# Background products in quarters with pauses behind each filled bank, and block 0's halves stored once

## The chip, the cores and the metric

The kernel runs on one core of a Trainium2 chip. The time is that of one execution on the device in microseconds (us), and it is compared by the median of several runs. One more execution is taken by the hardware profiler, and all lines of the profile come from that one. The engines are named as in the profile: PE is the matrix engine (PEld its weight loads), DVE the vector engine, ACT the scalar engine with its activation functions, POOL the general engine beside them, and SP the engine that issues most of the DMAs.

## The reference

The input x is 4096 tokens of 256 features. The kernel computes a causal attention with 16 heads of 16 features, its projection, a layernorm with the residual, and then a feed-forward part with ternary weights, again with layernorm and residual. All of it is in float32.

```python
def attn(x, w_attn, b_attn, w_proj, b_proj):
    q, k, v = jnp.split(x @ w_attn + b_attn, 3, axis=-1)      # 16 heads of 16
    logits = jnp.einsum('bhqd,bhkd->bhqk', q, k) * hd ** (-0.5)
    logits = jnp.where(causal[None, None, :, :], logits, -jnp.inf)
    weights = jax.nn.softmax(logits, axis=-1)
    return jnp.einsum('bhqk,bhkd->bhqd', weights, v) @ w_proj + b_proj
...
x = x + _layernorm(attn(_layernorm(x)))
x = x + _layernorm(ffn(_layernorm(x)))      # w1, w2: 1024 hidden; h1, h2: gelu; w3
```

## The kernel before

**Blocks, items, steps, units.** The 4096 queries are cut into 8 blocks j of 512 (`NB`, `QB`), the 16 heads into 4 groups g of 4 (`G`). An item is a pair (j, g), and the items run in order. `steps(j)` (L876) gives 4j + 3 steps to an item, one for each 128 keys up to the diagonal. A step has two units, each with the scores of two heads (128 keys by 512 queries), in two banks of PSUM; the last step of an item has one. That makes 32j + 20 units for a block and 1056 in all. The scores are computed with keys and queries as sums of a rounded part (hi) and a rest (lo).

**What a unit needs.** PE makes the scores s (`products`, L843), DVE takes one maximum mx over them (L852, which guards the shift of the softmax), ACT takes the exponential e_s (L859), POOL zeroes what is above the diagonal in the last steps (L866), and PE multiplies with the values (av, L930), a few units later. Scores have three tiles of two banks.

**Background work.** Beside the attention, other jobs advance a little in each step; `bg.even(every)` (called at the end of a step, if j < 2 or the step is ahead of the diagonal) moves them. A job is a generator that yields what it needs next: `PE` or `HALF` for a piece with matrix products, `ACT` for one with statistics on ACT, others for pieces that always run. The jobs are:

- `prep(j + 2)`, added at step 2 of group 1 of block j: loads x, layernorm by statistics on ACT (the tile junk, L203 and L211) and on POOL, transposes pt (L633), which ACT evicts to xT; then for c = 0, 1 the features pk and pq (L525), which ACT evicts to full (L534), which are split to hi and lo (L542, L544: on DVE for blocks 0 and 1, on POOL for later ones) and stored to DRAM (L549); then v (pv, L650, evicted by ACT at L658).
- `project(j)`: the projection py (L314, evicted by ACT at L332) of a finished block, then mean, spread and residual y (L224 and L351 on POOL).
- `norm_block(0)` in block 7, the entry to the feed-forward part.
- `halving`, in each fourth step: ternary weights are rounded in POOL (L1009 to L1012).

Background products use one PSUM bank (pool `ps_m`, one buffer). A bank of pk, pq, pv or py is filled in two halves: 128 by 512 for each of two parts of the contraction for pk and pq, two tokens' tiles by 256 for pv and py. The transposes fill a bank in one piece. While a bank is half full, only its own job may go on (`open`). The argument `every` is 1, 1, 2, 2, 3, 3, 3, 3 for the eight blocks: one half each `every` steps, an ACT piece in the step before.

**Keys and queries.** The stored halves of a block lie in DRAM as (head, 2, 2, 16, 512): each of hi and lo is stored twice, so that one load (`load_rows`, L557) brings a tile of 128 rows that has all combinations of hi and lo for two heads. `queries` and `keys` issue the loads on SP's queue. Before group 3 of a block the q of the next block must be stored (else `bg.step()` runs until it is), and before group 0 the whole prep of the block.

**Start.** Blocks 0 and 1 are loaded and normalised; then `biases()` scales the biases of q and k and adds the v bias through the projection to bp (products pb, L1106, which need the weights wp); then come the transposes of block 0, its pk and pq for c = 0, their stores, loads of the first two items, and the rest of block 0. `prep(1)` stands in the background from the first step on.

**The end.** After the attention the feed-forward part follows (L1358 and on, 672.10 us), which the change doesn't touch.

Of the kernel before, what the change touches and what calls it, by code (L numbers as in the profile page):

```python
# [3 lines left out]

# [6 lines left out]
F32 = mybir.dt.float32  # L11
F32R = mybir.dt.float32r
AF = mybir.ActivationFunctionType
ALU = mybir.AluOpType
# [3 lines left out]
P = 128  # L18
QB = 512
NT = QB // P  # L20
# [9 lines left out]
class Background:  # L30
# [6 lines left out]
    def __init__(self, beside=lambda: None):  # L37
        self.work = deque()
        self.beside = beside
        self.at = 0  # L40
        self.open = None

    def piece(self, gen):

# [47 lines left out]
                self.run(job)  # L92
            clear = clear and not job[4]

    def even(self, every):


        self.at += 1
        pe, act = not self.at % every, not (self.at + 1) % every
        for job in list(self.work):  # L100
            if job[3] in (self.PE, self.HALF):
                if pe and self.open in (None, job):
                    pe = False
                    self.run(job)
                    self.open = job if job[3] == self.HALF else None
            elif job[3] != self.ACT:
                self.run(job)
            elif act:
                act = False
                self.run(job)  # L110
# [7 lines left out]
def sandwich_kernel(  # L118
# [154 lines left out]
    def project(j, room):  # L273
# [35 lines left out]
        for half in range(0, NT, 2):  # L309
            ps = room.bank(f"py_{j}_{half}").rearrange("p (t f) -> p t f", t=2)  # L310
            for t in range(2):
                yield room.within(t)
                for c in range(DC):
                    nc.tensor.matmul(  # L314
                        ps[:, t, :],
                        lhsT=oT[:, c, (half + t) * P : (half + t + 1) * P],
                        rhs=wp[:, c, :],
                        start=(c == 0),
                        stop=(c == DC - 1),
                    )  # L320
# [83 lines left out]
    def attention(shared):  # L404
# [8 lines left out]
        with ExitStack() as actx:  # L413
# [22 lines left out]
            class Room:  # L436


                def within(self, n):
                    return Background.HALF if shared and n else Background.BESIDE  # L440

                def bank(self, name):
                    return bank(name) if shared else two_banks(name)[:, 0, :]
# [31 lines left out]
            def constants():  # L475
# [35 lines left out]


            halves_of = {
                (s, j): scratch.tile([H, 2, 2, HD, QB], F32, tag=f"{s}_{j}", name=f"{s}_{j}")
                for s in "kq"
                for j in range(NB)
            }
# [1 line left out]
            def features(j, s, c, engine):  # L519

                i = "qk".index(s)
                ps = room.bank(f"p{s}_{j}_{c}")
                for d in range(DC):
                    yield room.within(d)
                    nc.tensor.matmul(  # L525
                        ps,
                        lhsT=wqk[d][:, i * D + c * P : i * D + (c + 1) * P],
                        rhs=xTs[j][:, d, :],
                        start=(d == 0),
                        stop=(d == DC - 1),  # L530
                    )
# [12 lines left out]
                engine.tensor_tensor(lo.bitcast(F32R), full, hi.bitcast(F32R), ALU.subtract)  # L544
                for half, part in enumerate((hi, lo)):
                    for d in range(2):
                        at = (d, half) if i else (half, d)
                        queue = nc.gpsimd if shared and j < 2 and half else nc.sync
                        queue.dma_start(  # L549
                            out=halves_of[s, j][8 * c : 8 * (c + 1), at[0], at[1]], in_=part  # L550
                        )
                stored.add((s, j, c))

            def load_rows(tag, name, key, j, h):

                t = (piece if key == "k" else query)(tag, name, F32R)
                nc.sync.dma_start(  # L557
                    out=t.bitcast(F32),
                    in_=halves_of[key, j][h : h + 2].rearrange("h a b d n -> (h a b d) n"),
                )  # L560
                return t

            def query(tag, name, dtype):
# [10 lines left out]
            RING = 2 * NB  # L574
            kT, asked = {}, [0]

            def keys(n, c):

                for pr in range(2):
                    kT[n, c, pr] = load_rows(  # L580
                        f"k{asked[0] % RING}_{pr}", f"k{n}_{c}_{pr}", "k", c, 4 * (n % G) + 2 * pr
                    )
                asked[0] += 1

# [14 lines left out]
            def prep(j, engine=nc.gpsimd):  # L599
# [30 lines left out]
                for c in range(DC):  # L630
                    ps = room.bank(f"pt_{j}_{c}")
                    for t in range(NT):
                        nc.tensor.transpose(  # L633
                            ps[:, t * P : (t + 1) * P], xj[:, t, c * P : (c + 1) * P], ident
                        )
                    lent.append(True)
                    nc.scalar.copy(xT[:, c, :], ps)
                    if shared or c == DC - 1:
                        yield Background.PE
# [5 lines left out]
                for half in range(0, NT, 2):  # L645
                    ps = room.bank(f"pv_{j}_{half}").rearrange("p (t f) -> p t f", t=2)
                    for t in range(2):
                        yield room.within(t)
                        for c in range(DC):
                            nc.tensor.matmul(  # L650
                                ps[:, t, :],
                                lhsT=xT[:, c, (half + t) * P : (half + t + 1) * P],
                                rhs=wv[:, c, :],
                                start=(c == 0),
                                stop=(c == DC - 1),
                            )
# [443 lines left out]
            issued = now = 0  # L1100

            def biases():
                nc.vector.tensor_scalar(bqk[:, 0:DC], bqk[:, 0:DC], SCALE, None, ALU.mult)
# [145 lines left out]
    def feed_forward(halves, xT0, W):  # L1249
# [6 lines left out]
        with ExitStack() as fctx:  # L1256
# [10 lines left out]
                return ap.bitcast(F32R) if halves else ap  # L1267

            class Room:
                def within(self, n):  # L1270
                    return Background.BESIDE
# [236 lines left out]
```

## Time and profile before

| | us |
|---|---|
| median of 3 runs (2049.6 to 2054.11) | 2053.32 |
| profiled execution | 2048.42 |
| its span | 2046.5 |
| start, to the first maximum (39.81) | 39.81 |
| block 0 | 53.03 |
| block 1 | 75.08 |
| block 2 | 107.02 |
| block 3 | 147.81 |
| block 4 | 185.73 |
| block 5 | 216.71 |
| block 6 | 253.81 |
| block 7 | 295.40 |
| rest and feed-forward part | 672.10 |

A block is counted from its first maximum on DVE to the first of the next. In the span PE is busy for 89%, DVE for 79%, ACT for 68% and POOL for 27%, but in the feed-forward part PE has nearly all and DVE half. For the attention the lines that matter are those of DVE, ACT and PE in one step; a busy share does not show which one waits. Rows of a timeline have a start, a length from the first start to the last end of a run of equal instructions, the engine, the line, the operation and its tiles (result before the arrow), and in brackets the idle time ahead of it and what ended it. PE's rows are pipelined, so a record is longer than the spacing of two: the products of pv have records of 0.38 us and four of them take 1.06. Each float32 product makes two records.

### The profile page before, as it was taken

How to read it: one execution, taken by the hardware profiler on the slowest of the kernel's cores; microseconds unless marked ns; L12 is line 12 of the kernel's file. 1: busy time of each engine (PE TensorE's matmuls, PEld its weight loads, DVE VectorE, ACT ScalarE, POOL GpSimd, SP SyncE). 2: the span in 40 equal slices, each digit the busy share in tenths (PEclk: the TensorE clock that was granted, in tenths of full speed). 3: DMA queues.
4: the chain of work that ended last, by engine and by line, in shares of the span. 5: the costliest groups of instructions: out<-in, count | busy, mean ns of one | idle time of the engine just before them, and what ended most of it. 6: DMA issues, size and time to landing. Idle time of an engine off the chain costs nothing.

```text
span 2046.5 us, 28401 instructions
## 1 busy us (share of the span) xinstructions
PE 1825.3 (89%) x10518; PEld 932.5 (46%) x10518; DVE 1609.8 (79%) x1894; ACT 1399.2 (68%) x1598; POOL 552.2 (27%) x871
## 2 busy tenths in 40 slices
PE   4799989988888888888888887889999999999997
PEld 2333332322322322223222222228888888888886
DVE  3689998998999999999999999985546456465453
ACT  2699999999999999999999998982212222222221
POOL 3264545434435335333333110000120000000000
PEclk8899999999999999999999998999999999999999
DMA  6756645444235333553234213103100000000000
GB/s 168 229 179 219 191 133 180 147 154 159 98 131 183 116 103 124 161 163 115 76 136 156 98 44 101 63 9 114 53 11 21 15 7 21 1 21 21 1 11 15
DMA packets 134909, 202.09 MB, mean 99 GB/s; under 512 B 16064, under 2 KB 60736, under 8 KB 134752
## 3 DMA queue, kind: packets, MB, share of 16 engines
q1 hardware_dynamic: 130496, 194.56, 29.3%
q0 software_dynamic: 2480, 4.35, 1.0%
q8 instruction: 87, 1.43, 0.3%
q10 hardware_dynamic: 1776, 1.18, 0.3%
q14 instruction: 70, 0.57, 0.1%
HBM read 137.91 MB, written 62.13 MB: 98 GB/s over the span
## 4 chain that ended last, share of the span: by engine, by line
PE 46%; ACT 21%; DVE 19%; issue 6%; DMA 4%; POOL 2%; SPq 1%; ACTq 0%; POOLq 0%; DVEq 0%
PE z L1358 21%; ACT e_s L859 19%; DVE mx L852 18%; PE av L930 7%; PE s L843 7%; PE za L1358 3%; PE zb L1358 2%; PE pyf L1440 2%; DMA k<-k 1%; PE py L314 1%; PE pk L525 1%; PE pv L650 1%; PE pq L525 1%; ACT junk L211 1%; DMA q<-hiq 0%
## 5 line engine op out<-in xcount | busy, mean ns | idle before, releaser
L852 DVE TENSOR_REDUCE mx<-s 128x1 f32<-128x1024 f32 x1056 | 1219.8, 1217 | 72.1 <-PE s L843 66.6
L859 ACT ACTIVATE e_s<-s,shift 128x1024 f32<-128x1024 f32 x1056 | 1153.6, 1117 | 104.9 <-DVE mx L852 81.9
L843 PE MATMUL s<-q,k 64*128 64x512 f32 (+3 forms) x2304 | 517.7, 468 | 161.2 <-ACT e_s L859 144.7
L930 PE MATMUL av<-e_s,v 128*32 128x512 f32 (+2 forms) x4576 | 572.8, 575 | 7.9 <-POOL e_s L866 5.7
L843 PEld LDWEIGHTS s<-q,k 64*128 64x128 f32 x2304 | 208.9, 185 | 752.9 <-ACT e_s L859 652.2
L1425 ACT ACTIVATE fb<-z,sh 128x512 f32<-128x512 f32 x128 | 88.1, 689 | 364.8 <-PE z L1358 340.2
L1358 PE MATMUL z<-hb_0l,h 128*128 128x512 f32 x512 | 199.5, 390 | 0.0
L1358 PE MATMUL z<-hb_0h,h 128*128 128x512 f32 x512 | 199.5, 390 | 0.0
L866 POOL TENSOR_SCALAR_AFFINE_SELECT e_s<-e_s 128x256 f32<-128x256 f32 (+1 forms) x224 | 94.7, 440 | 337.4 <-ACT e_s L859 337.4
L233 POOL TENSOR_TENSOR rstd<-ve,neghalf 128x4 f32<-128x4 f32 (+1 forms) x22 | 20.8, 944 | 608.8 <-DVE ve L231 603.0
L930 PEld LDWEIGHTS av<-e_s,v 128*32 128x32 f32 x4576 | 97.2, 109 | 151.5 <-issue 116.1
L1325 DVE CAST hb_1h<-fb 128x512 fp32r<-128x512 f32 x64 | 27.4, 428 | 155.7 <-ACT fb L1425 155.7
L1402 ACT ACTIVATE sl<-za,s 128x512 f32<-128x512 f32 x64 | 44.0, 690 | 120.4 <-PE za L1358 60.9
L1325 DVE CAST hb_0h<-fb 128x512 fp32r<-128x512 f32 x64 | 28.1, 440 | 99.6 <-ACT fb L1425 99.6
L1358 PEld LDWEIGHTS z<-hb_0h,h 128*128 128x128 f32 x512 | 96.1, 188 | 20.0
L1358 PEld LDWEIGHTS z<-hb_0l,h 128*128 128x128 f32 x512 | 96.2, 188 | 19.8
L1011 POOL TENSOR_SCALAR wc<-wc 128x256 f32<-128x256 f32 x88 | 75.8, 861 | 7.8
L1010 POOL TENSOR_TENSOR wc<-wc,wh 128x256 f32<-128x256 f32 x88 | 64.3, 730 | 7.2
L1012 POOL TENSOR_TENSOR fit<-fit,wc 128x256 f32<-128x256 f32 x88 | 64.2, 730 | 7.3
L1009 POOL CAST wh<-wc 128x256 fp32r<-128x256 f32 x88 | 35.0, 397 | 108.4 <-DMA wc<-in_h_t_dram 75.9
L1440 PE MATMUL pyf<-w,hb_1l 128*128 128x256 f32 x256 | 61.8, 284 | 0.0
L1440 PE MATMUL pyf<-w,hb_1h 128*128 128x256 f32 x256 | 61.7, 283 | 0.0
(257 smaller groups left out, 1970.3 us busy)
## 6 DMA issues: line engine op xcount, KB each, us to landing
k<-k SPq DMA_DIRECT2D x288, 256.0 KB
q<-q SPq DMA_DIRECT2D x64, 256.0 KB
x<-in_x_dram SPq DMA_DIRECT2D x16, 512.0 KB
k<-hik SPq DMA_DIRECT2D x32, 256.0 KB
q<-hiq SPq DMA_DIRECT2D x32, 256.0 KB
wc<-in_h_t_dram SPq DMA_DIRECT2D x64, 128.0 KB
r_h<-wh SPq DMA_DIRECT2D x64, 128.0 KB
h<-r_h SPq DMA_DIRECT2D x32, 256.0 KB
```

What stands on the lines that cost most here:

```text
L843: nc.tensor.matmul(self.both[:, i, col : col + n], lhsT=kT[G * j + g, c, pr][r, tt * P : (tt + 1) * P], rhs=qT[j, g][pr][r, QB - n :], sta ...
L852: nc.vector.tensor_reduce(next(columns), self.both.rearrange("p a n -> p (a n)"), AX.X, ALU.max)
L859: nc.scalar.activation(e, self.both, AF.Exp, bias=shifts[j])
L866: nc.gpsimd.affine_select(out=here, in_=here, compare_op=ALU.is_ge, fill=0.0, base=0, pattern=[[0, here.shape[1]], [1, P]], channel_multip ...
L930: nc.tensor.matmul(self.av[h * HW : (h + 1) * HW, QB - n :], lhsT=vb[kt // NT][:, kt % NT, o : o + HW], rhs=of(es, h), start=(kt == 0 or k ...
L1010: nc.gpsimd.tensor_tensor(w, w, hi, ALU.subtract)
L1011: nc.gpsimd.tensor_scalar(w, w, 0.0, None, ALU.is_equal)
L1012: nc.gpsimd.tensor_tensor(fit, fit, w, ALU.mult)
L1325: nc.vector.tensor_copy(hi, full)
L1358: nc.tensor.matmul(ps, lhsT=w[c], rhs=single(part[:, c, :]), start=(c == 0 and i == 0), stop=(c == kc - 1 and i == parts - 1),)
L1425: nc.scalar.activation(h, z, AF.Gelu, scale=sc[:, oc : oc + 1])
L1440: nc.tensor.matmul(ps[:, 0:D], lhsT=single(part[:, c, t * P : (t + 1) * P]), rhs=(w3_r if halves else w3_sb)[:, c, :], start=(c == 0 and i ...
```

## The change

**The rate.** `even` takes four numbers. `products` is how many pieces with products may run in a step, `every` as before, `acts` the distance between ACT pieces, `rest` the pause behind a filled bank: for that many steps after the one that filled it, counted by `at`, no product is issued (a piece may run again when `at` reaches `at + rest`, so two whole steps and the one that filled lie ahead of it), and in the step that fills a bank no ACT piece runs. The call gives, for blocks 0 to 7, products 2, 2, 2, 1, 1, 1, 1, 1; every 1, 1, 2, 1, 1, 1, 1, 1; acts 1, 1, 2, 2, 3, 3, 3, 2; rest 0, 0, 0, 3, 3, 3, 3, 3.

**The quarters.** A bank is filled in four pieces. pk and pq are cut in two by columns (128 by 256) and each cut has its two parts of the contraction; pv and py have one product in a piece; the transposes have two pieces of two. The number of matrix instructions grows by that of the cut features, one more product for each half.

**Block 0.** Its hi and lo are stored once: q as (head, 2, 16, 512), k as (head, 16, 2, 512), and the loads repeat the rows by a broadcast; a key tile of block 0 is loaded by two DMAs of 128 KB in place of one of 256. For later blocks the layout in DRAM has another order of its dimensions with the same bytes and numbers of DMAs.

**The start.** The first two key loads go to POOL's queue. The scaling of the biases stays where it was, the products pb go behind the work on block 0. Ahead of the first attention step the background runs until k of block 1, c = 0, is stored: both transposes and pk of block 1. Before the norm of block 0 in block 7, `project(6)` is finished explicitly.

```diff
-    def even(self, every):
+    def even(self, products, every, acts, rest):
         self.at += 1
-        pe, act = not self.at % every, not (self.at + 1) % every
+        pe = 0 if self.at % every or self.at < self.rested else products
+        act = self.at % acts == 1 % acts
         for job in list(self.work):
             if job[3] in (self.PE, self.HALF):
-                if pe and self.open in (None, job):
-                    pe = False
+                while pe and job[3] in (self.PE, self.HALF) and self.open in (None, job):
+                    pe -= 1
                     self.run(job)
                     self.open = job if job[3] == self.HALF else None
+                    if rest and not self.open:
+                        pe, act, self.rested = 0, False, self.at + rest
...
             ps = room.bank(f"p{s}_{j}_{c}")
-                for d in range(DC):
-                    yield room.within(d)
+                cuts = 2 if shared else 1
+                for n, (cut, d) in enumerate(product(range(cuts), range(DC))):
+                    yield room.within(n)
+                    at = slice(cut * QB // cuts, (cut + 1) * QB // cuts)
                     nc.tensor.matmul(
-                        ps,
+                        ps[:, at],
                         lhsT=wqk[d][:, i * D + c * P : i * D + (c + 1) * P],
-                        rhs=xTs[j][:, d, :],
+                        rhs=xTs[j][:, d, at],
...
+                    queue = nc.gpsimd if shared and j < 2 and half else nc.sync
+                    kept = halves_of[s, j][8 * c : 8 * (c + 1)]
+                    for d in range(2) if j else ():
                         at = (d, half) if i else (half, d)
-                        queue = nc.gpsimd if shared and j < 2 and half else nc.sync
+                        queue.dma_start(out=kept[:, at[0], :, at[1]], in_=part)
+                    if not j:
+                        queue.dma_start(out=kept[:, :, half] if i else kept[:, half], in_=part)
...
+                elif key == "k":
+                    for i in range(2):
+                        rows = part[i : i + 1].rearrange("u d b n -> u (d b) n")
                         queue.dma_start(
+                            out=to[i * P // 2 : (i + 1) * P // 2],
+                            in_=rows.broadcast_to([2, 2 * HD, QB]),
                         )
+                else:
+                    rows = part.rearrange("h a (d u) n -> (h a d) u n", u=1)
+                    queue.dma_start(out=to, in_=rows.broadcast_to([P // 2, 2, QB]))
...
                     for t in range(NT):
+                        if shared and t == NT // 2:
+                            yield Background.HALF
                         nc.tensor.transpose(
...
-            biases()
+            nc.vector.tensor_scalar(bqk[:, 0:DC], bqk[:, 0:DC], SCALE, None, ALU.mult)
             while ("q", 0, 0) not in stored:
                 bg.piece(works[0])
             for n in range(2):
                 queries(*items[n])
-                keys(*chunks[n])
+                keys(*chunks[n], nc.sync if n or not shared else nc.gpsimd)
             while bg.piece(works[0]) is not False:
                 pass
+            biases()
             if shared:
                 bg.add(("prep", 1), works[1], PREP)
                 bg.work[0][3] = Background.PE
+                while ("k", 1, 0) not in stored:
+                    bg.step()
...
+                    bg.finish(("project", NB - 2))
                     bg.add(("norm", 0), norm_block(0, room, first_features), NORM)
...
-                        bg.even(1 + j // 2 - j // 6)
+                        bg.even(1 + (j < 3), 1 + (j == 2), (1, 1, 2, 2, 3, 3, 3, 2)[j], 3 * (j > 2))
```

More of the change, by code (lines that the diff above doesn't have):

```diff
@@ L2 @@
 from contextlib import ExitStack
-from itertools import chain, cycle
+from itertools import chain, cycle, product
 import concourse.bass as bass
@@ L41, in __init__ @@
         self.open = None
+        self.rested = 0
     def piece(self, gen):
@@ L311, in project @@
             for t in range(2):
-                yield room.within(t)
                 for c in range(DC):
+                    mark = room.within(DC * t + c, c > 0)
+                    if mark:
+                        yield mark
                     nc.tensor.matmul(
@@ L436, in attention, with within @@
             class Room:
-                def within(self, n):
-                    return Background.HALF if shared and n else Background.BESIDE
+                def within(self, n, fine=False):
+                    if shared:
+                        return Background.HALF if n else Background.BESIDE
+                    return None if fine else Background.BESIDE
                 def bank(self, name):
@@ L513, in attention @@
             halves_of = {
-                (s, j): scratch.tile([H, 2, 2, HD, QB], F32, tag=f"{s}_{j}", name=f"{s}_{j}")
+                (s, j): scratch.tile(
+                    [H, 2, HD, 2, QB] if j else [H, HD, 2, QB] if s == "k" else [H, 2, HD, QB],
+                    F32,
+                    tag=f"{s}_{j}",
+                    name=f"{s}_{j}",
+                )
                 for s in "kq"
@@ L545, in features, with load_rows @@
                 for half, part in enumerate((hi, lo)):
-                    for d in range(2):
+                    queue = nc.gpsimd if shared and j < 2 and half else nc.sync
+                    kept = halves_of[s, j][8 * c : 8 * (c + 1)]
+                    for d in range(2) if j else ():
                         at = (d, half) if i else (half, d)
-                        queue = nc.gpsimd if shared and j < 2 and half else nc.sync
+                        queue.dma_start(out=kept[:, at[0], :, at[1]], in_=part)
+                    if not j:
+                        queue.dma_start(out=kept[:, :, half] if i else kept[:, half], in_=part)
+                stored.add((s, j, c))
+            def load_rows(tag, name, key, j, h, queue=nc.sync):
+                t = (piece if key == "k" else query)(tag, name, F32R)
+                to, part = t.bitcast(F32), halves_of[key, j][h : h + 2]
+                if j:
+                    queue.dma_start(out=to, in_=part.rearrange("h a d b n -> (h a d b) n"))
+                elif key == "k":
+                    for i in range(2):
+                        rows = part[i : i + 1].rearrange("u d b n -> u (d b) n")
                         queue.dma_start(
-                            out=halves_of[s, j][8 * c : 8 * (c + 1), at[0], at[1]], in_=part
-                        )
[L552 to L560, printed above, removed]
+                            out=to[i * P // 2 : (i + 1) * P // 2],
+                            in_=rows.broadcast_to([2, 2 * HD, QB]),
+                        )
+                else:
+                    rows = part.rearrange("h a (d u) n -> (h a d) u n", u=1)
+                    queue.dma_start(out=to, in_=rows.broadcast_to([P // 2, 2, QB]))
                 return t
@@ L575, in attention, with keys @@
             kT, asked = {}, [0]
-            def keys(n, c):
+            def keys(n, c, queue=nc.sync):
                 for pr in range(2):
                     kT[n, c, pr] = load_rows(
-                        f"k{asked[0] % RING}_{pr}", f"k{n}_{c}_{pr}", "k", c, 4 * (n % G) + 2 * pr
+                        f"k{asked[0] % RING}_{pr}",
+                        f"k{n}_{c}_{pr}",
+                        "k",
+                        c,
+                        4 * (n % G) + 2 * pr,
+                        queue,
                     )
@@ L647, in prep @@
                     for t in range(2):
-                        yield room.within(t)
                         for c in range(DC):
+                            mark = room.within(DC * t + c, c > 0)
+                            if mark:
+                                yield mark
                             nc.tensor.matmul(
@@ L1102, in biases @@
             def biases():
-                nc.vector.tensor_scalar(bqk[:, 0:DC], bqk[:, 0:DC], SCALE, None, ALU.mult)
                 ps = two_banks("pb")[:, 0, 0:D]
@@ L1269, in feed_forward, with within @@
             class Room:
-                def within(self, n):
-                    return Background.BESIDE
+                def within(self, n, fine=False):
+                    return None if fine else Background.BESIDE
                 def bank(self, name):
```

## The prediction

> **What bounds the kernel now.** I read the list of costly groups first, then the timeline of DVE in blocks without disturbance, then the chain of waits beside it, then the table of windows by block, and last the places where a block loses much at once.
>
> ```profile
> L852 DVE TENSOR_REDUCE mx<-s 128x1 f32<-128x1024 f32 x1056 | 1219.8, 1217 | 72.1 <-PE s L843 66.6
> L859 ACT ACTIVATE e_s<-s,shift 128x1024 f32<-128x1024 f32 x1056 | 1153.6, 1117 | 104.9 <-DVE mx L852 81.9
> ...
> 1096.80 24.91 DVE L852 TENSOR_REDUCE mx<-s 128x1 f32<-128x1024 f32 x22
> ```
>
> Main attention is 1056 units, and each needs one maximum on DVE. Twenty-two of them run without a gap in 24.91 us: (24.91 - 1.22) / 21 = 1.13 us each, so a step of two units cannot be shorter than 2.26 us. The last column says that DVE's idle time ends when PE delivers scores. A stage is therefore measured by what it takes over 1.13 us for a unit. In block 4:
>
> ```profile
> 485.51 5.75 DVE L852 TENSOR_REDUCE mx<-s 128x1 f32<-128x1024 f32 x5 [0.21 <-PE s L843]
> 491.45 1.23 DVE L852 TENSOR_REDUCE mx<-s 128x1 f32<-128x1024 f32 x1 [0.19 <-PE s L843]
> 492.88 5.75 DVE L852 TENSOR_REDUCE mx<-s 128x1 f32<-128x1024 f32 x5 [0.20 <-PE s L843]
> ...
> 488.50 0.99 PE av L930 x8
> 489.49 0.43 PE s L843 x2
> 489.92 1.06 PE pv L650 x4
> 490.98 0.43 PE s L843 x2
> ```
>
> Here a background half is issued in every third step. The cycle from 485.51 to 492.88 is 7.37 us; three free steps are 6.78. So a half costs 0.59 us. The chain shows why: PE needs 0.43 + 0.99 + 0.43 = 1.85 us for a step, which leaves 0.41 of 2.26, and the half takes 1.06. It stands between two pairs of score products, so both following maxima come late.
>
> ```profile
> 0.00:39.81 39.81, 16.28 (x46) 8.40 (x46) 11.02 (x35) 6.37 (x9) 17.11 (x31) 0.96 0.60 156
> 39.81:92.84 53.03, 39.91 (x212) 17.32 (x212) 29.00 (x34) 30.02 (x41) 16.95 (x38) 0.77 0.72 222
> ...
> 36.00:54.00 18.00, 11.62 (x44) 5.44 (x48) 6.94 (x8) 6.33 (x7) 3.37 (x8) 0.53 0.73 253
> 74.00:85.00 11.00, 7.90 (x32) 3.59 (x32) 4.24 (x8) 5.02 (x8) 3.15 (x6) 0.54 0.86 259
> ...
> 23.86 9.77 DMA q<-hiq
> 35.21 5.63 DMA k<-k
> 40.88 0.82 PE s L843 x2
> ```
>
> Columns are length, then busy time of PE, weight loads, DVE, ACT, POOL, then granted clock, DMA share and GB/s. The start ends on the store of hiq and the load of k. Block 0 has 20 units, 22.6 us of maxima, and takes 53.03. In two stretches the clock is half, and the DMA engines are three quarters full. The blocks 3 to 7 have 116, 148, 180, 212 and 244 units; by the same table they last 147.81, 185.73, 216.71, 253.81 and 295.40, which is 82 us over their maxima. Followed step by step along DVE, 36.4 of these 82 stand at the 74 halves issued there (0.49 each; block 3 and steps that had slack lose less than 0.59), 7 at ACT's statistics (junk) in other steps, and the rest at fixed places: shift and its transpose, the reciprocals, the norm in block 7, and stalls like this one:
>
> ```profile
> 346.00 0.72 POOL L1012 TENSOR_TENSOR fit<-fit,wc 128x256 f32<-128x256 f32 x1
> 346.68 2.79 POOL L866 TENSOR_SCALAR_AFFINE_SELECT e_s<-e_s 128x256 f32<-128x256 f32 x7
> ...
> 347.15 2.28 PE L930 MATMUL av<-e_s,v 128*32 128x512 f32 x8 [1.82 <-POOL e_s L866]
> ...
> 350.20 3.49 DVE L852 TENSOR_REDUCE mx<-s 128x1 f32<-128x1024 f32 x3 [3.23 <-PE s L843]
> ```
>
> At the end of an item the diagonal selects queue on POOL behind rounding of features and weights; the product av waits, and DVE stands 3.23 us.
>
> **Quarters in blocks 3 to 7.** Before, a bank (two halves) loses 2 x 0.49 = 0.98 us. After, the built order has 138 spaced quarters, which fill 34.5 banks; eight transposed banks; and four quarters that are issued together ahead of (block 3, group 3), since q of block 4 isn't stored by then. The trace has no quarter. Its nearest rows are pv, two products of 256 columns in 1.06 us, and pk, one of 512 in 1.06: so a quarter is b = 0.53. Then a step with a quarter is 1.85 + 0.53 = 2.38, 0.12 over 2.26. Four in a row lose 0.48, and I add 0.11 for the eviction by ACT, which lies in a step of its own: c = 4 (b - 0.41) + 0.11 = 0.59 per bank. The three steps behind it are there to recover the lag. 34.5 x 0.59 = 20.4; transposes 8 x 0.15 = 1.2 (a whole one takes 0.59, two transposes 0.3, under the spare 0.41); the 7 of junk stays; the forced group 2.0 (4 x 0.53). Sum 30.6, against 36.4 + 7 = 43.4: **-12.8**. Bounds: quarters wholly hidden in the spare 0.41 and the score buffers, only evictions left, 5.2 + 10.2 = 15.4, which is -28; quarters that lose in proportion to the halves, 34.5 x 0.98 + 10.2 = 44, which is +0.6. I take the value between, since 0.53 exceeds 0.41.
>
> The Trainium skill speaks against the 0.53: "TensorE: Matmul & The Clock Gate", section "Back-to-back issue gap", gives a sustained spacing of about 81 ns at 128 columns and 131 at 512, so that half the columns cost much more than half. Between its two figures, 256 columns would be some 98 (an estimate from that page), and a quarter 1.06 x 98 / 131 = 0.79 in place of 0.53; the sum of all terms would then end near 2059. The rows of pv and pk, both 1.06, disagree with it at these sizes.
>
> **POOL's selects.** The slower rate changes what lies on POOL at each diagonal. Before, four ends lose 3.32 (block 3, group 1), 3.16 (4, 0), 1.65 (2, 3) and 0.85 (4, 3): 9.0. In the new order the last three have nothing queued in front; the first still has 7 us of rounding; four other ends (3, 2), (4, 1), (5, 2), (5, 3) have 4 to 4.6 us issued a step ahead, mostly done by then. I leave 3.5 + 0.5: **-5**. Bounds -8 (the first clears too) and 0 (the new ones take over).
>
> **Start.** Half of block 0's stores go (eight of 256 KB), four of which precede the first scores, and the bias product no longer heads PE's queue: it waits for wp until 12.24 and takes 2.05, so the transposes begin near 11, not 14.42. Against it: the transposes and pk of block 1 (0.87 + 0.67 + 2.00 by the start's own rows) are now ahead of the first score on PE, its rounding (0.43 + 0.69) ahead of the first maximum on DVE; lok_1_0 needs the lo buffer of k_0_1, whose store is on POOL behind the first key loads, moved there; a store from POOL lands in 7 us. They end near 36 to 37 by my chain; the first maximum then stands at 37.3, not 39.81: **-2.5**. Bounds: -6 (all 3.5 us of the wp wait and half of the 9.77 pass through, less the new products) and +3 (one more POOL landing is exposed, half of 7).
>
> **Block 0.** Work of block 1 is gone from its first steps, and PE isn't idle for 5 us before them. At full clock the 11.62 us of PE at 0.53 would be 6.2, the 7.90 at 0.54 would be 4.3: 5.4 + 3.6 = **-9**. Bounds: -13 (also 2.35 + 1.04 of waits for k at 79.45 and 92.30) and -3 (one third; the clock stays low). The keys' loads in two DMAs of 128 KB instead of one of 256 add 64 issues on SP, beside 0.4 us each at the start: 26 us of SP's queue over 1300, which has no work in most steps; if that cover is gone, a key comes 0.4 late, once per item.
>
> **Blocks 1 and 2.** Two quarters in one step are the same products as a half: **-0.5**, bounds -2 and +2 (the cut of features reloads weights, 0.19 a time, beside the products).
>
> `bg.finish(("project", 6))` finds it done. FFN isn't touched: 0.
>
> **Sum.** -12.8 - 5 - 2.5 - 9 - 0.5 = -29.8. The profiled execution took 2048.4, its span 2046.5; the median shown is 4.9 above it. 2048.4 - 29.8 + 4.9 = **2023.5**. Root of the squares of the distances to the bounds: 16 down (3.5, 4, 1.5, 3, 15.2), 17 up (5.5, 6, 2.5, 5, 13.4).
>
> **Rivals.**
> *Quarters bring nothing* (0.15). A step with a quarter has no slack, so every eviction and every junk becomes visible, and a bank loses what two halves did. For it: junk shows 7 us already. Against: y and v evictions behind a half cost nothing more. -17 + 0.6 = -16.4: **2037**.
> *Start and block 0 give nothing* (0.10). The key loads on POOL's queue come late and the clock stays at half. For it: POOL's landing of 7 us; against: fewer bytes. +3 - 3 + 2 - 5 - 12.8 = -15.8: **2037.5**. Both together (0.05): +3 - 3 + 2 - 5 + 0.6 = -2.4, **2051**, no change.
> *A lone quarter does not stream* (0.10), the slower side. Its two passes are records of 0.38 each; end to end they are 0.76, and the score pair behind takes 0.50 as after a wait, not 0.43: b = 0.83. Then c = 1.79, 34.5 x 1.79 + 10.2 = 72, +28.6 instead of -12.8: -17 + 28.6 = +11.6, **2065**. It decides from b = 0.75 (no change) and makes it slower from 0.78. Against it: pairs of two score products stream in 0.43.
> That the change doesn't do what it says I exclude: the quarters stand apart in the built order.
>
> **Numbers.** The forecast has 0.60; its own range is 2012 to 2034. With the rivals, 8 in 10 lie in 2007 to 2042. About 0.2% (4.1 us) can be told from no change: faster 0.85, same 0.05, slower 0.10.
>
> **What would show it.** In block 4, DVE rows should show four steps near 2.38 and then steps at 2.26, quarter records at 0.53 spacing, and a block shorter by about 6; no 3 us stall at the end of (4, 0); a forced group of pq ahead of (3, 3). In the start, the first maximum near 37 and a granted clock over 0.9 from 40 to 54. Wrong it is if a step with a quarter takes over 2.6 us, if the first maximum is later than 40, or if new waits for POOL's selects stand at (3, 2), (4, 1), (5, 2) or (5, 3).

## The result, and the profile after

The changed kernel takes 2109.45 us (median of 4 runs, 2104.31 to 2110.86), against 2053.72 for the kernel before: a ratio of 1.0269, 95% interval 1.0245 to 1.0293. It is slower by 56 us, where 30 us less were forecast. The profiled execution has a span of 2108.6.

The first view is the table of windows by block (length, busy times of PE, weight loads, DVE, ACT and POOL, then granted clock, DMA share, GB/s). The rows are the start, blocks 0, 1, 2, block 4, and a stretch of 8 us inside block 0.

```profile
0.00:51.17 51.17, 22.66 (x80) 15.58 (x80) 12.31 (x36) 8.23 (x12) 17.46 (x31) 0.91 0.48 126
51.17:113.55 62.38, 38.45 (x210) 19.38 (x210) 27.92 (x33) 26.10 (x31) 15.33 (x33) 0.74 0.49 144
113.55:210.50 96.95, 76.18 (x454) 30.31 (x454) 63.69 (x62) 69.95 (x95) 39.61 (x70) 0.88 0.48 149
210.50:334.50 124.00, 103.77 (x642) 37.64 (x642) 99.93 (x92) 100.36 (x126) 49.23 (x78) 0.93 0.51 162
478.90:661.60 182.70, 169.56 (x1046) 55.44 (x1046) 173.57 (x157) 171.50 (x196) 78.67 (x123) 0.98 0.45 139
...
100.50:108.50 8.00, 4.58 (x21) 2.21 (x22) 2.10 (x2) 2.23 (x2) 0.81 (x2) 0.50 0.13 49
```

By stage, after less before: start +11.4, block 0 +9.3, block 1 +21.8, block 2 +17.1, block 3 -3.5, block 4 -3.0, block 5 +7.1, block 6 -3.9, block 7 +5.8; in sum 62. So 59.6 of these 62 us lie in the start and the first three blocks, where the background rate is the same as before. The last row shows what it is like there: DVE works 2.1 of 8 us, the clock is at half, and the DMA engines are busy for a share of 0.13, as much as 2 of 16 at full use, at 49 GB/s. The waits say who is waiting (total, times, longest), for PE and DVE:

```profile
PE s L877 <- DMA k<-k: 20.6, 9, 3.4
...
DVE hik L557 <- DMA k<-hik: 15.8, 1, 15.8
DVE least L291 <- DMA sums<-avd: 10.7, 2, 5.4
```

The timeline of SP's queue in that time (start, time from the first issue to the end of the last, line):

```profile
96.57 9.37 SPq L579 DMA_DIRECT2D k<-k  x4
106.06 3.15 SPq L575 DMA_DIRECT2D k<-k  x2
111.49 0.32 SPq L992 DMA_DIRECT2D avd<-av_sb  x1
```

L579 is the load of a key tile of block 0 in two parts, L575 that of a key tile of block 1 in one. Four issues of L579 hold SP for 9.37 us, and the two behind them for 3.15. Most issues of L579 are short (median 0.51 us), and the kernel before had held ones too (four whole tiles in 6.29 us at 81.53); how the same four tiles fare without these loads is shown below. The store of the finished attention (avd) stands behind them, so its sums come late and DVE waits for them, 5 us in each of blocks 1 and 2.

The start ends on another thing. The chain of waits there (start, length, what):

```profile
35.64 2.76 SPq L579
38.40 0.05 issue
38.47 0.03 issue
38.50 11.54 DMA k<-hik
50.03 0.03 issue
50.08 0.04 issue
50.13 0.44 DVE hik L557
50.56 0.02 issue
50.59 0.69 DVE lok L559
51.28 2.28 DVE mx L886 x2
```

The first maximum stands on DVE behind hik of block 1, which waits until the store of block 0's second hik has left their common buffer; that store is issued behind the query and key loads on SP and then takes 11.54 us.

Last the quarters, in PE's timeline of block 4:

```profile
550.41 0.50 PE L877 MATMUL s<-q,k 64*128 64x512 f32 x2
550.84 0.70 PE L540 MATMUL pq<-xT,wqk 128*128 128x256 f32 x2
551.47 0.50 PE L877 MATMUL s<-q,k 64*128 64x512 f32 x2
551.89 1.06 PE L964 MATMUL av<-e_s,v 128*32 128x512 f32 x8
552.89 0.50 PE L877 MATMUL s<-q,k 64*128 64x512 f32 x2
553.32 0.70 PE L540 MATMUL pq<-xT,wqk 128*128 128x256 f32 x2
```

From 550.84 to 551.47 a quarter holds PE for 0.63 us, not 0.53, and the step from 550.84 to 553.32 is 2.48 long.

### The profile page after: what moved, and what is told of

Read it like the earlier page. It is cut to its first block, busy times and chain, and to the rows that moved or that the text cites. A ratio compares the mean times of both kernels' runs of the same rounds, so it can differ in the third digit from the quotient of the medians.

```text
span 2108.6 us, 28718 instructions
## 1 busy us (share of the span) xinstructions
PE 1868.0 (89%) x10646; PEld 959.3 (45%) x10646; DVE 1609.9 (76%) x1894; ACT 1399.1 (66%) x1598; POOL 553.9 (26%) x871
## 4 chain that ended last, share of the span: by engine, by line
PE 44%; ACT 23%; DVE 14%; DMA 8%; issue 7%; POOL 2%; SPq 2%; ACTq 0%; POOLq 0%; DVEq 0%
ACT e_s L893 21%; PE z L1395 20%; DVE mx L886 12%; PE av L964 7%; PE s L877 6%; PE za L1395 2%; PE zb L1395 2%; PE pyf L1477 2%; DMA k<-k 2%; DMA avd<-av_sb 2%; DMA k<-hik 1%; PE py L320 1%; PE pv L684 1%; DMA x<-x 1%; PE pk L540 1%
## 5 line engine op out<-in xcount | busy, mean ns | idle before, releaser
L877 PE MATMUL s<-q,k 64*128 64x512 f32 (+3 forms) x2304 | 537.3, 475 | 172.9 <-ACT e_s L893 136.5
L964 PE MATMUL av<-e_s,v 128*32 128x512 f32 (+2 forms) x4576 | 580.5, 583 | 7.4 <-POOL e_s L900 5.2
```

What stands on the lines that cost most here:

```text
L877: nc.tensor.matmul(self.both[:, i, col : col + n], lhsT=kT[G * j + g, c, pr][r, tt * P : (tt + 1) * P], rhs=qT[j, g][pr][r, QB - n :], sta ...
L964: nc.tensor.matmul(self.av[h * HW : (h + 1) * HW, QB - n :], lhsT=vb[kt // NT][:, kt % NT, o : o + HW], rhs=of(es, h), start=(kt == 0 or k ...
```

## The experiments

Three parts can be told apart: the storing and loading of block 0 (K), the new start (S), and quarters with pauses (Q). The kernel before has none of them, the changed one all. In the expectations, theory A is at first: the loads of block 0's keys have an outer dimension of 2 and so use few DMA engines; in later ones it is what they say. Stages are taken from one profiled execution each. All runs keep the changed order of the dimensions in DRAM. One of them, with quarters from block 4 on and otherwise the old start, has blocks 1 to 3 within 0.1 us of the kernel before, but its start at 42.51 instead of 39.81, so a difference of 2 or 3 us in a start alone can't be put down to one part.

**K alone.** From the changed kernel S and Q are taken back: the bias product stands ahead of the rest of block 0 again, and banks are filled in halves by the old `even`.

```diff
-                keys(*chunks[n], nc.sync if n or not shared else nc.gpsimd)
+                keys(*chunks[n])
...
-                while ("k", 1, 0) not in stored:
-                    bg.step()
...
-                        bg.even(1 + (j < 3), 1 + (j == 2), (1, 1, 2, 2, 3, 3, 3, 2)[j], 3 * (j > 2))
+                        bg.even(1 + j // 2 - j // 6)
```

> The kernel before with one part alone: block 0's halves stored once and its keys loaded by two DMAs with a repeated outer dimension of 2. Theory A (these loads use few DMA engines, about 50 GB/s as in 100 to 112 us of the changed kernel, and hold SP's queue): blocks 0 to 2 are longer by 35 to 55 us in sum, blocks 3 to 7 as before, total 2090 to 2110. Rival B (the new order of the start delays blocks 0 to 2): no change here, 2045 to 2056. Rival C (the quarters do it): no change here either.

Measured: 2138.84, ratio 1.0428 (1.0394 to 1.0462). The start is at 41.02, blocks 0 to 2 take 72.5, 104.4 and 124.8, which is 66.6 more than before. Blocks 3 to 7 were expected as before, but are 21 us longer: 2.5, 5.3 and 5.9 of it are new at three ends of items, and 7.0 at the norm of block 7, where DVE waits 6.9 us for a load of x that stands behind key loads on SP. K alone costs more than the whole change loses; A holds as to the main place, its size was guessed too low and its reach too short.

**S alone.** K and Q are taken back in the same way.

> The kernel before with the new start alone (bias product later, first keys on POOL's queue, transposes and pk of block 1 ahead of the first scores). Theory A: start and block 0 gain a little or lose a little, total 2040 to 2055. Rival B: the first maximum at 45 to 51 and blocks 0 to 2 longer by 30 to 48, total 2090 to 2110. Rival C: no change.

Measured: 2050.44, 0.9983 (0.997 to 0.9995). The first maximum comes at 49.42 as rival B said, but blocks 0 to 2 do not suffer (47.1, 76.0, 105.6). The new start moves 6 us of block 0 ahead of the first maximum and gains next to nothing.

**All but K.** Block 0 is stored twice, its tiles are loaded by one DMA:

```diff
-                    for d in range(2) if j else ():
+                    for d in range(2):
...
-                    if not j:
-                        queue.dma_start(out=kept[:, :, half] if i else kept[:, half], in_=part)
...
-                elif key == "k":
...
+                queue.dma_start(out=to, in_=part.rearrange("h a d b n -> (h a d b) n"))
```

> The changed kernel without its part on block 0: halves stored twice and loaded by one DMA of 256 KB. Theory A: the 60 us lost in the start and blocks 0 to 2 are gone but for 5, total 2035 to 2058. Rivals B and C: the total stays over 2090.

Measured: 2040.55, 0.9945 (0.9924 to 0.9966). The 69 us between this and the changed kernel are K: 5.7 in the start, 14.5, 20.8 and 18.2 in blocks 0 to 2, 11.4 in blocks 3 to 7. The place of the stretch shown above (there the 16th maximum starts at 100.15 and the 18th at 110.12) lies here between 84.91 and 89.90. The window around it, and the loads of the same four tiles on SP's queue, now read:

```profile
82.00:90.00 8.00, 5.92 (x32) 2.93 (x36) 2.45 (x3) 3.33 (x6) 0.82 (x2) 0.57 0.61 207
...
82.01 2.27 SPq L572 DMA_DIRECT2D k<-k  x4
```

The four tiles hold SP for 2.27 us and not for 9.37 + 3.15, and the two maxima take 4.99 us and not 9.97. The clock is near half here as well (0.57), so at this place it is no sign of K.

**Is it the shape of the load?** Two kernels ask this from both sides. In the first, block 0 stays stored once, and each key tile is loaded by four DMAs with 32 rows in front:

```diff
-                    for i in range(2):
-                        rows = part[i : i + 1].rearrange("u d b n -> u (d b) n")
-                        queue.dma_start(
-                            out=to[i * P // 2 : (i + 1) * P // 2],
-                            in_=rows.broadcast_to([2, 2 * HD, QB]),
-                        )
+                    for i in range(4):
+                        rows = part[i // 2].rearrange("d b n -> (d b) n")
+                        queue.dma_start(out=to[i * P // 4 : (i + 1) * P // 4], in_=rows)
```

> The changed kernel, but a key tile of block 0 is loaded by four DMAs of 64 KB, each with 32 rows as its outer dimension, in place of two of 128 KB with a repeated outer dimension of 2; stored once as before. Theory A (the outer dimension of 2 leaves most DMA engines idle): the waits of PE for k and the hold-ups on SP's queue in blocks 0 to 2 go, 40 to 65 of the 69 us between 2109 and 2041 come back, total 2035 to 2070, although there are twice as many DMAs. Rival D (the number of DMAs or their issue on SP's queue is what costs): slower still, 2130 to 2170. Rival E (the repeated reads of one place in DRAM cost): no change, 2100 to 2115.

Measured: 2040.16, 0.9938 (0.9923 to 0.9953). All of the loss is back with twice as many DMAs, so their number isn't the cost. For the first item, whose key loads are issued on POOL and whose landings the profile shows, a part of 128 KB lands after 7.2 us (median) in the changed kernel, a part of 64 KB after 4.1 here, and a whole tile of 256 KB after 5.0 in the kernel without K.

In the second, block 0 is stored twice, nothing is read repeatedly, and only a gap in DRAM keeps the outer dimension at 2 (on the kernel with free buffers, told below):

```diff
-                (s, j): scratch.tile([H, 2, HD, 2, QB], ...)
+                (s, j): scratch.tile([H, 2, HD + (s == "k" and not j), 2, QB], ...)
...
+                if key == "k" and not j:
+                    for i in range(2):
+                        queue.dma_start(
+                            out=to[i * P // 2 : (i + 1) * P // 2],
+                            in_=part[i, :, :HD].rearrange("a d b n -> a (d b) n"),
+                        )
```

> The kernel with free buffers (2035.8), block 0 stored twice; only its key tiles lie in DRAM with a gap, so that a tile is loaded by two DMAs of 128 KB whose outer dimension is 2, and nothing is read repeatedly. Theory A (an outer dimension of 2 leaves most DMA engines idle): blocks 0 to 2 are longer by 35 to 60, total 2080 to 2110. Rival E (the repeat costs): no change, 2034 to 2042.

Measured: 2109.82, 1.0281 (1.0263 to 1.0298); blocks 0 to 2 take 72.3, 97.2 and 124.5, 62 more than in the kernel with free buffers. A stretch of its block 0:

```profile
100.00:108.00 8.00, 4.64 (x21) 2.28 (x22) 2.31 (x2) 2.23 (x2) 0.81 (x2) 0.50 0.13 49
```

The same 0.13 and 49 GB/s without any repeated read: the outer dimension of 2 is the cause, and storing once is innocent of it. A third dimension in the pattern is not it either: the query loads of block 0 have one (64 by 2 by 512) and stand unchanged in the kernel that lost nothing.

**What holds up the start?** Two kernels. S without the products of block 1 ahead of the first scores (K and Q taken back, and the loop `while ("k", 1, 0) not in stored` left out):

> The kernel before with the new start, but without the transposes and pk of block 1 ahead of the first scores. Theory A (the first maximum waits behind hik_1_0 on DVE, which waits for the store of hik_0_1): the first maximum comes at 36 to 39 instead of 49.4, block 0 is back at 50 to 54, total 2045 to 2054, about as the new start as a whole. Rival F (the first key loads on POOL's queue or the bias product delay the first maximum): it stays at 45 or later.

Measured: 2048.33, 0.998 (0.9969 to 0.999). The first maximum comes at 38.71, block 0 takes 50.4. POOL's queue and the bias product don't delay it; the products of block 1 and what waits for them do.

And all but K, with buffers for hi and lo of (k, 1, 0) that are free then:

```diff
-                hi = piece(f"hi{i}", f"hi{s}_{j}_{c}")
+                own = shared and (s, j, c) == ("k", 1, 0)
+                hi = piece("k15_0" if own else f"hi{i}", f"hi{s}_{j}_{c}")
...
-                lo = piece(f"lo{i}", f"lo{s}_{j}_{c}")
+                lo = piece("k15_1" if own else f"lo{i}", f"lo{s}_{j}_{c}")
```

> The changed kernel with block 0 stored twice as before, and with hi and lo of (k, 1, 0) in two buffers that are free at that time (those of the last ring place of the keys), so that DVE's rounding doesn't wait for the store of hik_0_1. Theory A: the first maximum falls from 45.5 to 37 to 40, block 0 keeps 47 to 50, total 2030 to 2038. Rival F: no change, 2039 to 2045.

Measured: 2035.80, 0.992 (0.9907 to 0.9934), the fastest of all. The first maximum falls from 45.48 to 39.98 with nothing changed but the buffers. Its chain at that place has no DMA in front of hik any more:

```profile
38.19 0.70 ACT fullk L549
38.89 0.02 issue
38.91 0.44 DVE hik L558
39.35 0.02 issue
39.37 0.70 DVE lok L560
```

With both mendings, the loads of 32 rows and the free buffers:

> The changed kernel with both mendings: block 0 stored once with key loads of 32 rows, and free buffers for hi and lo of (k, 1, 0). Theory A: start plus block 0 at or under the 89.9 of the kernel with the buffers alone, rest the same, total 2030 to 2040. If the repeated loads still delay others (as the clock's fall in block 4 group 3 with stored-once kernels hints), 2037 to 2043.

Measured: 2037.57, 0.9926 (0.9911 to 0.9942), not to be told from the last. Start and block 0 take 90.76 here and 89.89 there: half the stores of block 0 are worth nothing that shows.

**What is a quarter worth?** By small losses the sum over all steps of blocks 3 to 7 is meant that lose under 0.9 us each, from the step's first maximum to that of the next, over 1.13 us for a unit. Quarters and pauses alone in all blocks stop in a deadlock and have no time, so the first run has them from block 4 on (the pieces of pt, pv and py have the same condition as `cuts`):

```diff
-                        bg.even(1 + j // 2 - j // 6)
+                        block[0] = j
+                        bg.even(1, 1 + (j in (2, 3)), (1, 1, 2, 2, 3, 3, 3, 2)[j], 3 * (j > 3))
...
+                cuts = 2 if shared and block[0] > 3 else 1
```

> The kernel before with quarters and pauses alone, from block 4 on. Theory A: blocks 0 to 3 as before within 2 us; in blocks 4 to 7 the small losses fall by 3 to 7 and the select's stall of block 4 group 0 (3.16) goes: total 2041 to 2050. If the quarters save nothing (a quarter at 0.63 of PE and 2.47 a step, a bank at 1.0): only the select's 3 us, 2048 to 2053.

Measured: 2061.64, 1.0039 (1.0026 to 1.0053): slower, against both readings. The small losses fall from 52.3 to 44.2, but two large ones stand against them: 7.55 us at the last step of (4, 0) and 6.45 at (4, 1, 7), that is block 4, group 1, step 7. At the first, POOL's timeline reads:

```profile
465.97 1.28 POOL L307 TENSOR_TENSOR oo<-oo,xT0lo 128x512 f32<-128x512 f32 x1 [2.35 <-DMA xT0lo<-invd]
...
473.67 0.72 POOL L1036 TENSOR_TENSOR fit<-fit,wc 128x256 f32<-128x256 f32 x1
474.37 0.56 POOL L228 TENSOR_SCALAR y<-y,mvy,rstd 128x256 f32<-128x256 f32 x1
475.01 0.72 POOL L357 TENSOR_TENSOR y<-y,x 128x256 f32<-128x256 f32 x1
475.69 2.81 POOL L890 TENSOR_SCALAR_AFFINE_SELECT e_s<-e_s 128x256 f32<-128x256 f32 x7
```

POOL has waited 2.35 us for a DMA; then the projection's work (oo, then y) and a rounding of weights stand in front of the diagonal's selects, nearly ten us without a pause, and av waits 6.0 us for them. At the second place, the chain of waits runs over a load of x that lands after 8.01 us. Where such work meets a diagonal goes with the alignment of the jobs, that is, how many steps earlier or later a job runs, and the start of the changed kernel gives another one: with S and Q that end loses 0.01 (all but K), and with S alone, in halves, 0.00.

Halves in the place of quarters from block 3 on, two in successive steps and then a pause, on the kernel with free buffers (pt, pv and py again as `cuts`):

```diff
-                cuts = 2 if shared else 1
+                cuts = 1 if block[0] > 2 or not shared else 2
...
-                        bg.even(1 + (j < 3), 1 + (j == 2), (1, 1, 2, 2, 3, 3, 3, 2)[j], 3 * (j > 2))
+                        bg.even(1 + (j < 3), 1 + (j == 2), (1, 1, 2, 2, 3, 3, 3, 2)[j], 5 * (j > 2))
```

> The kernel with free buffers (2035.8), but halves and not quarters from block 3 on, two in successive steps and then a pause, at the same rate of a bank in six steps. If each insertion of products between two score pairs costs PE about 0.2 beside its columns (records start 0.32, 0.22, 0.22, 0.31 apart in a half, 0.32 and 0.31 in a quarter), two halves hold PE 2.12 and four quarters 2.52, but the halves exceed the slack of a step by 0.65 each: a bank loses 1.0 to 1.3, total 2034 to 2045. If the quarter itself brings the gain, a bank loses 1.3 and more, total 2042 to 2052.

Measured: 2056.05, 1.0013 (1.0003 to 1.0023), above both ranges. The small losses are 57.6 us, with quarters 45.5 (kernel with free buffers). At the same rate a bank in quarters is cheaper than one in two adjoining halves. This is 12 of the 20 us between the two kernels; large losses at other steps, such as 4.98 instead of 1.32 at the end of (3, 1), make up the rest in part.

The quarters in another place, between av and the second unit's scores:

```diff
                         if n or p:
                             unit.finish()
+                        if j > 2 and unit is units[0] and p < NT * j:
+                            bg.even(1, 1, (1, 1, 2, 2, 3, 3, 3, 2)[j], 3)
```

> The kernel with free buffers (2035.8), but from block 3 on the quarters stand between av and the second unit's scores, not between two score pairs (the position in the step of all background work moves with it). If the 0.2 per insertion comes from the change of weights between products of different shape, it stays (0.6 to 0.66 for a quarter), total 2030 to 2042. If it comes from the score pairs that lie on both sides, a quarter falls to 0.45 to 0.55 and steps with quarters to 2.3 to 2.4: total 2020 to 2032.

Measured: 2056.85, 1.0017 (1.0007 to 1.0027), above both ranges. A quarter still takes 0.63, from 491.21 to 491.84:

```profile
490.22 1.06 PE L952 MATMUL av<-e_s,v 128*32 128x512 f32 x8
491.21 0.70 PE L540 MATMUL pq<-xT,wqk 128*128 128x256 f32 x2
491.84 0.73 PE L865 MATMUL s<-q,k 64*128 64x512 f32 x4
```

So the extra is the same in both places. The place matters in another way: here the small losses are 68.2 us, probably because each quarter delays the second unit of its own step; the other background work moves with the quarters, and no run tells the two apart.

## Why the prediction was wrong

**The step that failed** is in the paragraph on block 0: "The keys' loads in two DMAs of 128 KB instead of one of 256 add 64 issues on SP, beside 0.4 us each". The load was priced by its issue alone, and its transfer was taken to go as before, since its bytes are the same. Its shape is not: `broadcast_to([2, 2 * HD, QB])` puts a dimension of 2 in front, and while such DMAs run the DMA share is that of 2 engines, at 49 GB/s. The parts with the 32 rows in front, and the gap in DRAM, show it from both sides. The Trainium skill has this rule in "DMA: Bandwidth & Descriptors", section "Rules for kernel authors", and names a leading broadcast as its example: an outermost dimension of c below 16 confines the DMA to at most c engines. The trace agrees, with a DMA share of 0.13. It cost 69 us, more than twice all the gains that were forecast. PE's own waits for keys are 23.3 us in the whole program, against 7.1 without K, and the rest came in good part by way of others: SP's queue held for 9 us and more, avd and x loads late, and a granted clock of 0.88 and 0.93 in blocks 1 and 2 (1.00 in both without K).

**Start** (forecast -2.5): +11.4 in the changed kernel. About 5.7 of it is K. 5.5 is the wait of hik_1_0 for its buffer. The prediction looked at this chain, but at lok and POOL's landing; hik has the same kind of buffer, and its store sits on SP's queue behind the loads. With both gone the first maximum is at 39.98 and the start gives nothing: the products of block 1 fill what the bias product set free (without them it is at 38.71). One reading was off by a row as well: the load of k that lands at 40.84 belongs to the second maximum; the first was held by its own key load until 38.98.

**Block 0** (-9): +9.3; without K -5.2, with the buffers free -3.1 at a start as before. In the kernel with free buffers the clock rose nearly as said: in the stretch from 36 to 54 us it is 0.91 there, 0.53 before (in the changed kernel 0.67). But the time did not follow the clock. Start and block 0 together are 89.88 us there, against 92.84 before, so -3.0 in place of -11.5. Its row of that stretch, and the chain of waits of its block 0, show what bounds it:

```profile
36.00:54.00 18.00, 12.58 (x70) 7.48 (x70) 8.69 (x12) 5.88 (x8) 4.94 (x11) 0.91 0.73 222
...
40.56 10.78 DMA q<-hiq
...
58.10 7.40 DMA k<-k
...
72.98 7.26 DMA k<-k
```

A store holds the buffer of the next hiq for 10.78 us, and then loads of k follow that lie behind it on SP's queue: 25.4 of 49.9 us are three transfers. The step that failed here is reading the half clock as the cause, where PE also waited for transfers; a kernel with shorter transfers and the same clock wasn't tried.

**Blocks 1 and 2** (-0.5): +38.9, and without K -0.1. The term was right; the loads broke it.

**Quarters** (-12.8): by the same split of the steps, the small losses of blocks 3 to 7 go from 52.3 to 43.5, -8.8 (-6.5 without K). Right in sign, too large. The term b was mis-sized: 0.63 us for 0.53. The starts of the records say why in the kernel before already: the four of a half of pv lie 0.32, 0.22, 0.22 and 0.31 apart, so a half is four times 0.22 and 0.19 at its ends. The prediction divided 1.06 by two and so the ends as well; two records are 0.44, and the ends 0.19. The rival on the slower side had put 0.83, and its point of decision, 0.75, wasn't reached. The 0.79 that the prediction estimated from the skill's figures erred to the other side by more, but half the columns did cost more than half the time, as it said there. With b = 0.63 the formula c = 4 (b - 0.41) + 0.11 gives 0.99 for a bank, as much as two halves, and 34.5 x 0.99 + 10.2 - 43.4 = +1 for the whole term, so the prediction's own sum does not explain the gain that there is. The banks measured in block 5 lose 0.65 to 1.05 each, since the first quarter behind a pause costs 0 to 0.2 and not the 0.22 of the later ones; the steps around them seem to lose less to junk, which was not counted one by one.

**Selects** (-5): the four ends named lose 1.4 us instead of 9.0 (1.34 in block 3 group 1, under 0.05 at the others): -7.6. None of the four new ends showed a stall of its own. But the cause was not the slower rate of the quarters, and the number is luck: with S alone, at the old rate in halves, the same four ends lose 1.30, 0.00, 0.00 and 0.80; with S but without the products of block 1 ahead of the first scores 3.53, 3.57, 1.65 and 0.86, as before; and quarters from block 4 alone leave 7.55 at the end of (4, 0). So most of this gain goes with the work that the start moves ahead, which shifts later jobs by some steps.

**The forced group of pq** (2.0): the end of (3, 2) goes from 1.63 to 3.39, +1.8.

**New in blocks 4 to 7** and not forecast: 3.3 us in (4, 3, 2) and (4, 3, 3) at a granted clock of 0.58, 4.7 at (5, 1, 8) where ACT's statistics wait 4.1 us for x, and 7.3 at the norm, where DVE waits 7.2 us for x. Without K 0.4, 1.3 and 0.0 are left of them. The last two come from the slow loads: the kernel with the gap in DRAM has them too (5.8 and 7.4), the one with loads of 32 rows 1.3 and 0.0. The first does not: the kernel with loads of 32 rows has it (3.3), the one with the gap 0.4; its cause stays open.

**Of the signs announced**, the free end of (4, 0) and the forced pq were seen, steps with a quarter took 2.48 instead of 2.38, block 4 is shorter by 3.0 (5.9 without K, where 6 was said), and the granted clock from 40 to 54 us was 0.58, where over 0.9 was said. The first maximum was at 51.2, later than the 40 that was to prove the prediction wrong. Neither the rivals nor the range, which ended at 2042, held a case in which the transfers themselves become slow. The best kernel, with K out and the buffers free, gains about 16 us of the 29.8 forecast (2035.80 against 2051.65 in the same session).

## What to carry to other kernels

A DMA is priced by its shape, not by its bytes: look at the outermost dimension of each changed access pattern, and at what else waits in that queue. Cut a product into pieces only after reading the starts of single records, since each insertion pays its ends again (0.19 us here). Before work is moved ahead on an engine that keeps its order, list the buffers that it writes and when their last readers, stores included, will be done.

## What the runs showed of the hardware

- While key loads with an outer dimension of 2 ran, the DMA share was 0.13 at 49 GB/s; at the same place with whole tiles it was 0.61 at 207. The issues of the same four tiles held SP's queue for 12.5 us in the first case and 2.27 in the second.
- Inserting a product between products of other shapes costs PE 0.19 to 0.20 us beside its columns: 0.63 for two records of 256 columns, 1.06 for four of them and also for two of 512. The transposes have 0.15 at their ends (mostly 0.37 for two, 0.59 for four). It is the same between two score pairs and behind av.
- Work that was moved by some steps could gain or lose 3 to 7 us at one diagonal (0.04 in one kernel, 3.16 and 7.55 in others), nearly as much as all quarters bring.
